# The third batch's layer-0 feed-forward moved into the rotary attention of a four-layer kernel on Trainium2

## The chip, the cores and the metric

The kernel runs on one core of one Trainium2 chip. Five engines work beside each other, each with its own queue of instructions: TensorE (PE), VectorE (DVE), ScalarE (ACT), GpSimd (POOL) and SyncE (SP). The metric is device microseconds for one launch. A profiled execution gives a trace, and the page and the answers made from it; all times of single instructions below come from such a trace.

## What is computed

Four batches of 1024 tokens with 128 channels go through four layers. Every layer has the same frame: half a feed-forward, an attention, half a feed-forward, each added to the residual X. Cut to what matters here:

```python
# layer 0: MoE with 8 experts, two of them for a token (gelu), and a small attention over the heads of one token
# layer 1: dense feed-forward and softmax attention with rotary positions, 16 heads of 8 channels
def _L1_ffn_ref(x, w_gate, w_up, w_down):      # HIDDEN = 384
    h = silu(x @ wg.T) * (x @ wu.T)
    return h @ wd.T
def _L1_attn_ref(x, w_qkv, w_out, b_out):
    q, k = q * cos + rotate_half(q) * sin, k * cos + rotate_half(k) * sin
    attn = softmax(q @ k.T * scale)            # over all 1024 tokens of the batch
    return (attn @ v) @ w_out + b_out
# layer 2: MoE and a linear attention; layer 3: RWKV
```

Each part is applied to the normalized X (mean removed, divided by the standard deviation over the 128 channels). The dense feed-forward (half of it, a factor 0.5) ends the kernel's layer-0 stage: it is the first feed-forward of layer 1, and the program issues it batch by batch as soon as a batch's second MoE is combined. In the program it is called `last`.

## The kernel before

**Data.** X[b] is a tile of 128 channels by 1024 tokens in SBUF for each batch b = 0 to 3. "The third batch" is b = 2; b = 3 is the last. A half is 512 tokens.

**Layer 0 and its planner.** Layers 0, 2 and 3 are written as generators of tasks in lanes (`lanes`). In layer 0 the tasks are `route` (which tokens go to which expert), `experts` (blocks of 128 slots; each loads its expert's weights on SP (L834), gathers tokens on POOL, runs two groups of matmuls and scatters the result on POOL (L878)), `combine` (adds the two experts' results to X), the attention, `last(b)`, and `prepare` (the rotary attention's queries, keys and values of batch 0). The second MoE has a group for each batch. The operations are noted down, not issued: `Score.order` then schedules all of them with a table of estimated costs for each engine, and `play` issues them in this order. All of these have the line L296 in the profile, except where a helper issues by itself (L834 and L878). The order of all five engines in the layer is therefore one plan, and any task that is taken out makes it a different one.

**`last(b)`**, which is `l1_ffn` (L1023), does two halves of: a center matmul (X minus its mean), Square and copy, variance matmuls, square root and reciprocal, four transposes that spread the scale over the tokens (`spread`), the product xn, then for three chunks of 128 hidden channels a gate matmul, `AF.Silu`, an up matmul and a product on DVE, and at the end three down matmuls that accumulate and an addition to X. Each matmul of 512 float32 columns shows as two passes.

**The last batch is treated differently.** `macaron` keeps batch 3's second `combine` out of layer 0 (`self.late`, L1767), and `last` is made for the batches 0 to 2 only. Both run later, inside the rotary attention.

**The rotary attention, `l1_attn`** (L1142). Ahead of its loop, POOL fills the rings of padded queries and keys (`l1_rings`, L1076 and L1080) and the value tiles (L1334), and SP loads the first queries and keys from DRAM (`l1_spread`, L1138). The loop at k runs over 256 steps and 11 more:
- `greatest`, steps 0 to 255: for two pairs of heads each, two score matmuls into a `two` tile (64 rows of contraction, two PSUM buffers) and one maximum on DVE (L1181). A step has two such reduces.
- `shifted` after each eighth step: the maxima are turned by four transposes and written beside the queries.
- `scores`, from step 11 on: the score matmuls again, with the maximum subtracted, into an `s` tile (three PSUM buffers), and the exponential on ACT (L1209).
- `values`, one step later: products with the values; `normalized` at the end of each 8 steps.
- at the end of each step, every generator in `running` is advanced by one piece. `coming` prepares batches 1 to 3 (`l1_prepare`, from step 64b - 61), a piece in every third step; `late` runs, from step 10 on and again a piece in every third step, batch 3's `combine` and its feed-forward `feed`. These, too, take their PSUM from the three `s` buffers.

PE is in program order here; the other engines' instructions are ordered by the framework.

**`feed(b, hf)`** is `last` for half a batch, as ten pieces: the center matmul, Square (L1287) and copy; four variance matmuls with root and reciprocal; the spread and xn; for three chunks a gate piece (matmul, Tanh, and (tanh + 1) times gate in one DVE operation, L1307) and an up piece (matmul and product, L1312); the three down matmuls with the addition to X (L1317). The silu is made of tanh: g (tanh(g/2) + 1) is twice silu(g), and the factor at the end is 0.25, not 0.5. Tanh and the exponential need no change of ACT's function table between them in the trace; Sqrt does.

Of the kernel before, what the change touches and what calls it, by code (L numbers as in the profile page):

```python
# [20 lines left out]
B, S, D = 4, 1024, 128  # L21
# [536 lines left out]
class Macaron:  # L558
# [583 lines left out]
    def l1_attn(self, m, c1, f):  # L1142
# [6 lines left out]
        with ExitStack() as ctx:  # L1149
# [16 lines left out]
            def values_of(n):  # L1166
                b, g4 = n // 4, n % 4
                nc.gpsimd.tensor_copy(
                    va[n % RING][:, :, :, 1 : 1 + HD],
                    self.ring["vd"][b % 2][:, :, 32 * g4 : 32 * g4 + 32].rearrange("p t (h d) -> p t h d", d=HD),  # L1170
                )

            def greatest(unit, pair, nm):
                n, (c, it, h) = unit // 16, (unit // 8, unit % 8 // 2, unit % 2)
                at = (c % 2 * 4 + it) * P
                s = two((P, 2, HALF))
                for j in (1, 0):
                    g = 2 * pair + j
                    self.mm(s[:, j, :], of(qz, n, g)[:, at : at + P], of(kz, n, g)[:, h * HALF : (h + 1) * HALF])
                    yield  # L1180
                v.tensor_reduce(nm[:, it, h, 2 * pair : 2 * pair + 2], s, AX.X, ALU.max, negate=True)  # L1181

            def shifted(chunk, nm):
                top, n = tops[chunk % 2], chunk // 2
                least = self.t(wp, [P, 4, 4], "least")
                v.tensor_tensor(least, nm[:, :, 0, :], nm[:, :, 1, :], ALU.min)
                v.tensor_copy(top[:, :, :, 0].bitcast(F32R), least)
                v.tensor_tensor(top[:, :, :, 1], least, top[:, :, :, 0], ALU.subtract)
                yield
                tp = two((P, HALF))  # L1190
                for i in range(4):
                    nc.tensor.transpose(
                        tp[:, i * P : (i + 1) * P], top[:, i].rearrange("p g r -> p (g r)"), self.c0["ident"]
                    )
                sh = self.t(wp, [P, HALF], "sh", F32R)
                nc.scalar.copy(sh, tp)
                for g in range(4):
                    z = of(qz, n, g)[32:34, chunk % 2 * HALF : (chunk % 2 + 1) * HALF]
                    nc.sync.dma_start(out=z.bitcast(F32), in_=sh[32 * g : 32 * g + 2, :].bitcast(F32))
                yield  # L1200

            def scores(unit, pair, es):
                n, jt, at = unit // 16, unit % 8, unit // 8 % 2 * HALF
                for j in range(2):
                    g = 2 * pair + j
                    o = self.t(p2, [P, HALF], "s")
                    self.mm(o, of(kz, n, g)[:, jt * P : (jt + 1) * P], of(qz, n, g)[:, at : at + HALF])
                    e = es[g] = self.t(wp, [P, HALF], "e", bufs=10)
                    nc.scalar.activation(e, o, AF.Exp, scale=scale)  # L1209
                    yield  # L1210

            def values(unit, o, es, half):
                n, jt = unit // 16, unit % 8
                c = slice(half * HALF // 2, (half + 1) * HALF // 2)
                for g in range(4):
                    self.mm(
                        o[32 * g : 32 * g + 32, c], va[n % RING][:, jt, g, :], es[g][:, c],
                        start=jt == 0 and half == 0, stop=jt == NT - 1 and half == 1,
                    )
# [101 lines left out]
            def chain(*parts):  # L1321
                for first, part in parts:
                    while at < first:
                        yield
                    for _ in part:
                        yield
                        yield
                        yield

            at = -1  # L1330
            late = [(10, part(b, hf)) for part in (combine, feed) for b in self.late for hf in range(2)]
            coming = [(64 * b - 61, self.l1_prepare(p2, "s", prep, m, c1, b)) for b in range(1, B)]
# [6 lines left out]
            running, nms, pending, o = [chain(*coming)], {}, None, None  # L1339
            for k in range(units + LEAD + 1):  # L1340
                at = k
                first = k if k < units else None
                second = k - LEAD if 0 <= k - LEAD < units else None
                if k % 16 == 2 and RING <= k // 16 + 1 < 4 * B:
                    self.l1_spread(k // 16 + 1)
                    values_of(k // 16 + 1)
                if k == 1:
                    running.append(chain(*late))
                if first is not None and first % 8 == 0:
                    nms[first // 8] = self.t(wp, [P, 4, 2, 4], "nm", bufs=3)  # L1350
                es = {}
                for pair in range(2):
                    top = greatest(first, pair, nms[first // 8]) if first is not None else iter(())
                    part = scores(second, 1 - pair, es) if second is not None else iter(())
                    for one in (part, top, top, part, top):
                        next(one, None)
                    if pending:
                        unit, then = pending
                        if unit % 8 == 0 and pair == 0:
                            o = self.t(pa, [P, HALF], "o")  # L1360
                        values(unit, o, then, pair)
                if pending and unit % 8 == 7:
                    running.append(normalized(unit // 8, o))
                pending = (second, es) if second is not None else None
                if first is not None and first % 8 == 7:
                    running.append(shifted(first // 8, nms[first // 8]))
                running = [r for r in running if next(r, self) is not self]
            while running:
                running = [r for r in running if next(r, self) is not self]
# [408 lines left out]
    def layer0(self, moe, m, right, enter, ffn, l1a, c1):  # L1778
        m["wqkvc"] = self.centered(m["wqkv"], 3 * D)
        spare = enter(self.rings, "l1vd", 1)  # L1780
        self.ring["vd"] = [self.t(spare, [P, NT, D], f"vd{i}") for i in range(2)]
        pa, pf = enter(right, "l0a"), enter(right, "l1f0", side="left")
        side = self.side

        def more(route):
            attn = lambda b, *after: (f"middle{b}", after, lambda: self.l0_attn(side, pa, m, b))
            last = lambda b: (f"last{b}", (f"combine1{b}",), ffn(pf, side, b))
            prepare = ("prepare", ("last0",), lambda: self.l1_prepare(side, "bank", pf, l1a, c1, 0))
            return (
                [*[route(0, g) for g in groups[0]], *[attn(b, f"combine0{b}") for b in range(B)]],  # L1790
                [route(1, g, *(f"middle{b}" for b in g)) for g in groups[1]],
                [last(0), prepare, *[last(b) for b in range(1, B - 1)]],
            )

        groups = [(0,), (1,), (2, 3)], [(b,) for b in range(B)]
        marks = {(n, g): f"_{n}{g[0]}" for n in range(2) for g in groups[n]}
        aside = [(0, (1,)), (0, (2, 3)), (1, (0,)), (1, (1,)), (1, (2,))]
        self.macaron("l0", moe, AF.Gelu, groups, marks, more, [(1, B - 1)], aside)
# [112 lines left out]
```

## Time and profile before

| | |
|---|---|
| time, median of 8 runs (range) | 2475.01 us (2468.7 to 2481.79) |
| profiled execution: time | 2474.69 us |
| profiled execution: span, first to last instruction | 2472.9 us |
| mean granted TensorE clock | 0.953 |
| busy: PE, DVE, ACT, POOL | 2193.0, 1766.5, 1546.9, 1093.2 us |
| layer 0 | from 0 to 702.5 us |
| rotary attention, first and last reduce | 703.05 and 1485.7 us |
| layers 2 and 3 | the rest |

The span is what lies between the first and the last instruction; the time of the execution is 1.8 us longer. Busy time is an average over stages in which different engines are full, so the sum says little about one of them: for that, the profile cuts the span into 40 equal slices of 61.8 us (a digit is the busy share in tenths), and windows of any length can be asked for. An idle time in brackets behind an instruction, with an arrow, is how long its engine was idle ahead of it, and what ended that. `out<-in` are the program's names of the tiles.

### The profile page before, as it was taken

The numbers are of one execution on the slowest core, as the hardware profiler recorded it, in microseconds if no ns is written. First come the engines' busy times: TensorE is split into PE (matmuls) and PEld (weight loads), VectorE is DVE, ScalarE is ACT, GpSimd is POOL, SyncE is SP. The second block draws the span as 40 slices with busy tenths as digits, with TensorE's granted clock in tenths as the row PEclk, the third lists the DMA queues.
The fourth block names the chain that finished last, engine by engine and source line by source line (L and its number), as shares of the span: only waits on it lengthen the run. The fifth ranks groups of instructions, "written<-read, shape, count | busy, mean of one in ns | idle before, by whom it ended". The sixth has DMA issues, their size and how long they took to land. (4 is left out here: it accounts for less than half of the span.)

```text
span 2472.9 us, 44544 instructions
## 1 busy us (share of the span) xinstructions
PE 2193.0 (89%) x15631; PEld 1396.8 (56%) x15631; DVE 1766.5 (71%) x2891; ACT 1546.9 (63%) x3903; POOL 1093.2 (44%) x1140
## 2 busy tenths in 40 slices
PE   5879787988979999999999999988998978689986
PEld 4878776776744334334333334578887968433332
DVE  4488979886458887998988992542656542398995
ACT  5567675855537776787788886654554554456643
POOL 2778876578622201210320000077454567255553
PEclk8989998999969999999999999998998989899998
DMA  6977766567731101110220000278666689200000
GB/s 200 294 225 243 227 205 193 161 194 235 229 84 57 53 19 36 55 51 19 69 69 19 25 3 11 74 249 267 217 195 198 207 268 284 81 0 5 5 9 17
DMA packets 135694, 312.40 MB, mean 126 GB/s; under 512 B 20752, under 2 KB 70032, under 8 KB 135344
## 3 DMA queue, kind: packets, MB, share of 16 engines
q1 hardware_dynamic: 110320, 253.28, 31.9%
q0 software_dynamic: 25152, 56.28, 8.2%
q8 instruction: 125, 2.05, 0.3%
q14 instruction: 97, 0.79, 0.1%
HBM read 259.86 MB, written 49.09 MB: 125 GB/s over the span
## 5 line engine op out<-in xcount | busy, mean ns | idle before, releaser
L1181 DVE TENSOR_REDUCE nm<-two 128x2 f32<-128x1024 f32 x512 | 622.9, 1223 | 70.6 <-PE s L601 42.8
L1209 ACT ACTIVATE e<-s 128x512 f32<-128x512 f32 x1024 | 558.2, 598 | 132.9 <-PE s L601 119.3
L296 POOL DMA_INDIRECT e_xg<-rows,g_source x333 | 379.7, 1140 | 437.4 <-DVE g_target L296 221.9
L296 ACT ACTIVATE e_h<-bank,e_w 128x128 f32<-128x128 f32 x1332 | 383.6, 377 | 266.7 <-PE bank L296 113.4
L878 POOL DMA_INDIRECT res<-e_y,g_target x333 | 370.6, 1113 | 184.7 <-issue 45.8
L296 PE MATMUL bank<-e_x,e_w 128*128 128x128 f32 x2664 | 387.3, 286 | 38.5 <-DMA e_w<-in_l0m_dram 22.1
L296 PE MATMUL bank<-e_w,e_h 128*128 128x128 f32 x2664 | 390.5, 283 | 8.9 <-ACT e_h L296 8.9
L601 PE MATMUL s<-qz,kz 64*128 64x512 f32 x1024 | 383.0, 449 | 2.9 <-ACT e L1209 2.9
L296 PEld LDWEIGHTS bank<-e_x,e_w 128*128 128x128 f32 x2664 | 349.0, 200 | 60.0 <-issue 31.9
L601 PE MATMUL two<-kz,qz 64*128 64x512 f32 x1024 | 360.2, 460 | 6.8 <-DVE nm L1181 6.7
L296 PEld LDWEIGHTS bank<-e_w,e_h 128*128 128x128 f32 x2664 | 352.9, 198 | 20.5 <-ACT e_h L296 12.7
L601 PE MATMUL o<-e,va 128*32 128x256 f32 x4096 | 328.7, 392 | 7.6 <-ACT os L1226 7.5
L601 PEld LDWEIGHTS s<-qz,kz 64*128 64x128 f32 x1024 | 157.6, 186 | 205.0 <-issue 98.0
L601 PEld LDWEIGHTS o<-e,va 128*32 128x32 f32 x4096 | 81.6, 108 | 191.9 <-issue 173.6
L1140 POOL MEMSET qz<- 2x1024 f32 x52 | 49.1, 945 | 309.0 <-PE s L601 306.8
L296 ACT ACT_TABLE_LOAD x124 | 159.1, 1283 | 12.8 <-PE bank L296 9.8
L296 PE MATMUL bank<-c,e_xg 128*128 128x128 f32 x333 | 93.6, 292 | 78.8 <-DMA e_xg<-rows,g_source 69.6
L296 DVE TENSOR_TENSOR e_y<-bank,e_w 128x128 f32<-128x128 f32 x202 | 57.5, 286 | 142.5 <-PE bank L296 131.9
L601 PEld LDWEIGHTS two<-kz,qz 64*128 64x128 f32 x1024 | 143.2, 189 | 25.3 <-DVE nm L1181 21.9
L296 DVE COPY e_x<-bank 128x128 f32<-128x128 f32 x162 | 45.8, 286 | 135.6 <-PE bank L296 134.1
L1119 POOL TENSOR_TENSOR h<-h 128x512 f32<-128x512 f32 x12 | 15.4, 1283 | 226.8 <-DVE h L1115 172.5
L296 PEld LDWEIGHTS bank<-c,e_xg 128*128 128x128 f32 x333 | 48.5, 147 | 97.2 <-issue 41.1
(316 smaller groups left out, 3454.3 us busy)
## 6 DMA issues: line engine op xcount, KB each, us to landing
e_w<-in_l0m_dram SPq DMA_DIRECT2D x177, 578.0 KB
e_w<-in_l2m_dram SPq DMA_DIRECT2D x156, 578.0 KB
c_y<-res SPq DMA_DIRECT2D x30, 512.0 KB
stack<-s POOLq DMA_DIRECT2D x48, 256.0 KB
rows<-g_xt SPq DMA_DIRECT2D x16, 512.0 KB
qz<-stack SPq DMA_DIRECT2D x64, 128.0 KB
kz<-stack SPq DMA_DIRECT2D x64, 128.0 KB
e_xg<-rows,g_source POOLq DMA_INDIRECT x333
```

Of the source, the lines that this page charges most:

```text
L296: return call(*a, **k)
L601: self.nc.tensor.matmul(out, lhsT, rhs, start=start, stop=stop)
L878: ins = real.gpsimd.indirect_dma_start(out=res[:, :], out_offset=at(target[:, k : k + 1]), in_=y, in_offset=None)
L1119: nc.gpsimd.tensor_tensor(whole, turned[:, 0, :], turned[:, 1, :], ALU.add)
L1140: self.nc.gpsimd.memset(z[at + 32 : at + 34, :].bitcast(F32), 0.0)
L1181: v.tensor_reduce(nm[:, it, h, 2 * pair : 2 * pair + 2], s, AX.X, ALU.max, negate=True)
L1209: nc.scalar.activation(e, o, AF.Exp, scale=scale)
```

## The change

`last` is made for the batches 0 and 1 only, and a generator `first_feeds` runs `feed` for batch 2, both halves: 20 pieces. It is put into `running` at k = 0 without `chain`, so it is advanced in every step, from step 0 to step 19. The operations are those of `feed` above, so the silu of batch 2 is made of tanh. Batch 3's `late` work keeps its place, and so does the preparation of the batches 1 to 3; batch 2's begins at step 67, which is behind the pieces.

```diff
@@ in l1_attn
+            def first_feeds():
+                for hf in range(2):
+                    yield from feed(B - 2, hf)
+
             at = -1
             late = [(10, part(b, hf)) for part in (combine, feed) for b in self.late for hf in range(2)]
...
                 if k == 1:
                     running.append(chain(*late))
+                if k == 0:
+                    running.append(first_feeds())
@@ in layer0
-                [last(0), prepare, *[last(b) for b in range(1, B - 1)]],
+                [last(0), prepare, *[last(b) for b in range(1, B - 2)]],
```

## The prediction

> **What bounds the kernel now.** I read four views, in this order. First the busy tenths in 40 slices, 61.8 us each, to find which engine is full in which stage.
>
> ```profile
> PE   5879787988979999999999999988998978689986
> DVE  4488979886458887998988992542656542398995
> POOL 2778876578622201210320000077454567255553
> PEclk8989998999969999999999999998998989899998
> L1181 DVE TENSOR_REDUCE nm<-two 128x2 f32<-128x1024 f32 x512 | 622.9, 1223 | 70.6 <-PE s L601 42.8
> ```
>
> Counted from 0, slice 11 (680 to 742 us) is the border of layer 0 and the rotary attention: POOL falls from 6 to 2, and the granted clock is at 6 tenths there and nowhere else. In the rotary attention behind it (slices 12 to 23) PE is at 9 throughout and DVE at 7 to 9. A step of it needs two reduces of L1181 (512 of 1223 ns), and neighbouring reduces start 1.23 us apart when nothing else is there: a bare step is 2.46 us.
>
> Second, the windows around the border: from the end of batch 3's attention of layer 0 (602 us) to rotary step 26, and a late stretch. Columns: stretch, its length, then busy us (instructions) of PE, PEld, DVE, ACT, POOL, the granted clock, the DMA share, GB/s.
>
> ```profile
> 602.00:628.00 26.00, 23.34 (x96) 13.15 (x95) 18.34 (x62) 20.42 (x54) 24.53 (x27) 1.00 0.47 127
> 655.00:687.00 32.00, 25.62 (x211) 23.92 (x210) 5.88 (x23) 15.07 (x55) 23.83 (x29) 0.97 0.92 282
> 687.00:705.00 18.00, 15.72 (x115) 13.49 (x113) 5.56 (x13) 6.75 (x24) 7.84 (x16) 0.95 0.54 151
> 705.00:736.00 31.00, 23.21 (x67) 11.16 (x67) 24.34 (x29) 8.00 (x16) 3.91 (x9) 0.51 0.10 28
> 1100.00:1300.00 200.00, 197.19 (x1726) 79.91 (x1724) 176.08 (x188) 157.81 (x293) 37.77 (x49) 1.00 0.17 51
> ```
>
> From 655 to 687 the transfers are at 0.92: batch 3's expert weights come at the speed of the DMA engines, and PE is idle for 6.4 of 32 us. From 705 to 736 nothing is full, at half the clock: there is room in the first rotary steps, and a clock that makes PE's work cost double. Third, POOL and PE at the end of layer 0:
>
> ```profile
> 632.56 0.99 POOL L296 DMA_INDIRECT e_xg<-rows,g_source  x1 [4.40 <-DVE g_far L296]
> 690.88 0.97 POOL L878 DMA_INDIRECT res<-e_y,g_target  x1 [3.59 <-DVE e_y L296]
> 701.40 0.97 POOL L878 DMA_INDIRECT res<-e_y,g_target  x1 [3.97 <-DVE e_y L296]
> ...
> 685.96 0.45 PE L296 MATMUL bank<-c,e_xg 128*128 128x128 f32 x1 [3.44 <-DMA e_xg<-rows,g_source]
> 699.44 1.13 PE L296 MATMUL bank<-e_x,e_w 128*128 128x128 f32 x8 [1.28 <-DMA e_w<-in_l0m_dram]
> 702.51 1.04 PE L601 MATMUL two<-kz,qz 64*128 64x512 f32 x4
> ```
>
> Each line ends with the idle time before it and what ended it. The rotary attention begins (702.51) right behind the last expert matmul, and what PE waits for on the way there is a gather, then a weight; no wait is on the feed-forward that moves. Last, DVE in the first rotary steps:
>
> ```profile
> 703.05 9.14 DVE L1181 TENSOR_REDUCE nm<-two 128x2 f32<-128x1024 f32 x8
> 713.55 6.88 DVE L1181 TENSOR_REDUCE nm<-two 128x2 f32<-128x1024 f32 x6 [1.36 <-PE two L601]
> 721.79 3.48 DVE L1181 TENSOR_REDUCE nm<-two 128x2 f32<-128x1024 f32 x3 [1.36 <-PE two L601]
> ...
> 728.93 2.35 DVE L1181 TENSOR_REDUCE nm<-two 128x2 f32<-128x1024 f32 x2 [1.22 <-PE two L601]
> 734.00 1.23 DVE L1181 TENSOR_REDUCE nm<-two 128x2 f32<-128x1024 f32 x1 [2.72 <-PE two L601]
> ```
>
> Eight reduces follow each other without a gap: even here, where neither exp nor values run, the reduces set the pace (2.26 us a step). Each idle time of DVE stands where a background piece of batch 1's preparation held up PE (a center matmul 1.36 each, the transposes 1.22, the sixteen variance passes 2.72).
>
> **What the change removes in layer 0.** The feed-forward of batch 2 is 18 matmuls (592 ns at the median, two passes each, 0.86 us from start to start: 15.5 us), two center matmuls (1.7), the variance passes (2.0) and the spreads (1.7): about 21 us of PE, with ten DVE operations of 0.69 us and ten ACT operations of about 0.6. Its PE work lies at 619 to 656, its late down matmuls at 654.5, 686.2 and 695.6. The Silu table loads (1283 ns each) go too; they lie on ACT beside waits.
>
> How much earlier the last expert matmul comes depends on what else is late. The whole of layer 0 is ordered anew by its planner. Comparing the two orders of instructions: in the changed kernel DVE has 498.4 us of work ahead of the last attention's addition to X (493.0 before), and 16.9 us from there to the last routing's g_source (25.5 before), so the routing is ready sooner. But POOL has 10 scatters and a gather of batch 2 left at that point, where before it had 2 scatters: 9 more operations at 1.27 us (0.97 and a 0.30 us issue gap), 11.4 us. The 24 ring fills of POOL (0.95 us each) stand there as before: all ahead of batch 3's first gather, 19 of them in the changed order. So:
> - If POOL's queue decides: between 602 and 704.9 it has 20.0 us of idle gaps longer than 0.6 us. All of them filled, with 11.4 us of work added, it ends 8.6 us sooner. If the gaps stay as they are, less the 11.4 us that fill them, it ends when it ended: 0.
> - If PE's queue decides: 21 us sooner.
> - Transfers are for the first: at 0.92 of the DMA engines, 32 us of this stretch cannot be shortened by taking PE work from it; and 20 of the first 24 loads of qz and kz now stand behind the last weight on SP (6 before), 128 KB each. At 282 GB/s one takes 0.46 us, and the first reduce needs four, so up to 2 us, which I leave in the bounds.
> I take **-7 us** for layer 0, next to the POOL bound; bounds 0 and -21.
>
> **What it adds in the rotary attention.** Twenty pieces, one a step, at steps 0 to 19. A step's length is the distance between the first reduces of neighbouring steps. The trace has the same function for batch 3, later, at full clock; steps with one of its pieces and nothing else, less the bare 2.46: center 3.52 (+1.06), variance 3.77 (+1.31), the step after it with the table back 3.90 (+1.44), spread 3.03 (+0.57), gate 4.32 and then 2.27 (+1.67), up 3.52 (+1.06), the three downs 5.24 (+2.78). One half of the batch: 1.06 + 1.31 + 1.44 + 0.57 + 3 x 1.67 + 3 x 1.06 + 2.78 = 15.35 us.
>
> Second half of the batch, steps 10 to 19. Scores begin at step 11, so that row applies: +15.35. Step 12 is 5.32 us now, because the four spreads of batch 1's preparation run at half clock; step 30 has the same spreads at full clock in 3.05. With 128-row matmuls in steps 3 to 10 the clock may be back by then: -2.3. If center and variance at steps 10 and 11, ahead of the scores, find room as in the first half, another 2.4 goes. I take **+13** (10.7 to 15.4).
>
> First half, steps 0 to 9, which take 31.0 us now (703.0 to 734.0). No row shows these pieces here, so two bounds. If the clock stays full, PE has the room: two reduces take 2.26 us and the four passes of a step about half of it. What counts is DVE: eight operations of 0.69 and a reciprocal of 0.19 are 5.7 us, and the DVE idle times shown above, 1.36 + 1.36 + 1.22 + 2.72 = 6.7 us, would go, since they come from PE at half clock: about 0. If the clock is half throughout, each of the ten big matmuls costs what the center matmul costs at step 3 (3.70 - 2.27 = 1.43), 14.3, and the variance and spread pieces about 2.4: +17. What does the clock do? The window 702.4 to 705.8 has PE busy for 1.94 of 3.40 us, and from 705.8 the clock is 0.50; a window with 1.99 of 3.40 inside layer 0 (589.8 to 593.2), filled by full-height matmuls, keeps 1.00. So the 64-row matmuls of the reduces seem to count for less, and the added 128-row pieces could hold the clock part of the time. I take the middle, **+8**.
>
> A rule of the Trainium skill stands against the row here. Its page "TensorE: Matmul & The Clock Gate", section "HAM oscillation — how this bites in real kernels", lets the clock fall only after PE has been idle for over some 3.4 us; in the trace the longest idle time of PE ahead of the fall is 0.78 us, and it falls. By the rule the clock would stay full, the first half would cost nothing, and the sum would be +6 instead of +14; the measurement decides.
>
> **Sum.** -7 + 8 + 13 = +14 us. The profiled run took 2474.69 us (span 2472.9), the median of the eight runs is 2475.01: the same within 0.4 us. Forecast 2489 us. After step 20 the order of instructions is unchanged, and so is what follows; nothing there gives the time back, because from there on PE is busy for 197 of 200 us.
>
> **Rivals.**
> 1. *Faster.* Layer 0's end is bound by PE's queue and the routing ahead of it, not by POOL. For: the routing's g_source has 8.6 us less DVE work ahead of it, and the first gather (632.56) waited 4.40 us for that chain; DVE is idle from 590.7 to 601.3 ahead of the last addition. Against: the DMA share of 0.92 and the 11.4 us on POOL. Price: the 21 us of PE work and those 4 to 8.6 us, 25 to 30 off layer 0, and +21 in the rotary attention: 2475 - 6 = 2469. It decides from the point where the first rotary matmul starts before 702.5 - 21 = 681.5 us.
> 2. *The clock holds.* The added matmuls keep the clock up from step 0: the first half costs nothing, the second its low end. -7 + 0 + 11 = +4: 2479. For: the full-height window above. Against: of the pieces of steps 0 to 2, where the clock falls, only the center matmul is big.
> 3. *Half clock and no gain.* POOL's added work eats all of layer 0's gain, and the clock stays low to step 12: 0 + 17 + 13 = +30: 2505. For: the slice with clock 6, and 19 x 0.95 + 11.4 = 29.5 us of POOL work ahead of batch 3's gathers. Against: 20 us of POOL's idle time.
> That the pieces don't run where they are put can be excluded: the order on PE, which is manual here, has them at steps 0 to 19.
>
> **Chances.** Forecast (+8 to +22) 0.50; faster 0.22; the clock holds 0.16; half clock and no gain 0.12. This kernel's measurement tells about 0.2% (5 us) from no change. Of the faster case 0.04 lies within that, of the clock case 0.11, the rest of it above: faster 0.18, same 0.15, slower 0.67. The range: the bounds of the sum are -21 + 0 + 11 = -10 (2465) and 0 + 17 + 15 = +32 (2507). I let it reach from 2465 to 2503; left out are the rest of rival 1 (0.08) and the upper part of rival 3 (0.07). The forecast's own range is 2483 to 2497.
>
> **What would show it.** Right: the first rotary matmul at 693 to 699 us; the first reduce of step 20 some 83 us behind the first rotary matmul (62.5 now); gaps of POOL ahead of the scatters smaller than now. Wrong: the first rotary matmul before 681 (rival 1); a granted clock over 0.9 from the start to step 10 (rival 2); the start at 702 or later with the clock at 0.5 past step 12 (rival 3). Also wrong would be a difference in the profile behind step 25, where I cost nothing.

## The result and the profile after

The changed kernel takes **2491.07 us** at the median of 15 runs (2485.35 to 2497.25); the kernel before takes 2474.98 us beside it (43 runs). The ratio is 1.0066, with a 95% interval of 1.0055 to 1.0076: 16 us slower. The forecast was 2489 us. The sum came out within 2 us; its term for layer 0 did not, as the trace shows.

The profiled execution took 2494.53 us (span 2492.7), 3.5 us over its median, where that of the kernel before lay on its median. So of the 19.8 us between the two spans some 3.5 are chance. First the slices of the page:

```profile
PE   5888887978789999999999999997997978689986
DVE  4487899795268887888998992552656652398995
POOL 2778776566822201220220000067554567255553
PEclk7999988989889999999999999999998989899998
L1181 DVE TENSOR_REDUCE nm<-two 128x2 f32<-128x1024 f32 x512 | 623.2, 1222 | 67.6 <-PE s L601 45.7
```

Slice 11 (now 686 to 748 us) no longer stands out: the granted clock is at 8 tenths there, not 6. The reduces cost what they cost. Slice 10 of POOL is at 8 (it was 6): its queue is full ahead of the border. Then the windows. The columns are stretch, length, busy us (instructions) of PE, PEld, DVE, ACT and POOL, clock, DMA share, GB/s:

```profile
602.00:628.00 26.00, 24.08 (x204) 21.97 (x203) 14.97 (x61) 17.71 (x68) 23.47 (x31) 1.00 0.85 259
628.00:633.00 5.00, 0.00 (x0) 0.00 (x0) 0.00 (x0) 0.00 (x0) 4.66 (x6) 0.71 0.76 268
633.00:655.00 22.00, 15.28 (x101) 14.34 (x102) 2.34 (x9) 7.84 (x29) 17.80 (x21) 0.73 0.53 147
655.00:687.00 32.00, 25.51 (x186) 24.09 (x186) 9.09 (x30) 13.84 (x48) 25.24 (x30) 0.87 0.90 285
```

The second line carries the reading of layer 0: for 5 us PE, DVE and ACT do nothing at all, and POOL alone works. What it works on, and who waits for it, the timelines of DVE, POOL and PE show:

```profile
625.54 0.23 DVE L296 SCALAR_TENSOR_TENSOR g_source<-g_w,g_far 128x23 uint32<-128x23 f32 x1
...
626.72 0.95 POOL L1080 MEMSET kz<- 32x1024 f32 x1
627.83 0.96 POOL L878 DMA_INDIRECT res<-e_y,g_target  x1 [0.16 <-issue]
629.00 2.90 POOL L1080 MEMSET kz<- 32x1024 f32 x3
632.07 0.96 POOL L878 DMA_INDIRECT res<-e_y,g_target  x1 [0.17 <-issue]
633.07 0.95 POOL L1080 MEMSET kz<- 32x1024 f32 x1
634.17 0.98 POOL L296 DMA_INDIRECT e_xg<-rows,g_source  x1 [0.16 <-issue]
...
636.71 0.48 PE L296 MATMUL bank<-c,e_xg 128*128 128x128 f32 x1 [9.09 <-DMA e_xg<-rows,g_source]
...
702.89 0.73 PE L601 MATMUL two<-kz,qz 64*128 64x512 f32 x4
```

The last routing is ready at 625.5 us, 6.6 us sooner than before (632.1). But its first gather is issued at 634.17, behind ring fills and batch 2's last scatters in POOL's queue; before, it came at 632.56. PE waits 9.09 us for it, and the first rotary matmul comes at 702.89 us, where it was 702.51. **Layer 0 has gained nothing.**

In the rotary attention (steps counted from the first reduce; 703.43 us now) the steps 0 to 9 take 34.8 us, where they took 31.0, and the steps 10 to 19 take 42.0, again for 31.0. Together +14.8. From step 20 to the last reduce it is 721.9 for 720.7. The DVE timeline of the first steps:

```profile
703.43 5.75 DVE L1181 TENSOR_REDUCE nm<-two 128x2 f32<-128x1024 f32 x5
709.09 0.17 DVE L1296 RECIPROCAL frstd<-fstd 128x4 f32<-128x4 f32 x1
...
710.29 0.67 DVE L1301 TENSOR_TENSOR f_xn<-f_xc,s 128x512 f32<-128x512 f32 x1
710.88 4.78 DVE L1181 TENSOR_REDUCE nm<-two 128x2 f32<-128x1024 f32 x4
715.58 0.68 DVE L1307 SCALAR_TENSOR_TENSOR f_s<-f_t,s 128x512 f32<-128x512 f32 x1
...
729.20 2.36 DVE L1181 TENSOR_REDUCE nm<-two 128x2 f32<-128x1024 f32 x2 [0.65 <-PE two L601]
...
734.14 0.20 DVE L1101 RECIPROCAL p_r<-p_std 128x8 f32<-128x8 f32 x1 [1.53 <-ACT p_std L1100]
737.60 0.69 DVE L1317 SCALAR_TENSOR_TENSOR x<-s,x 128x512 f32<-128x512 f32 x1 [3.26 <-PE s L601]
```

To 729 us DVE stands without a gap, between reduces and the pieces' own operations: the center matmuls at steps 3 and 6, each of which stopped it for 1.36 us before, stop it no more, since the clock is at 1.0. (In a second profile of the same kernel the clock was at 0.5 in just these two steps, and they took 4.1 and 4.2 us, not 2.4 and 2.9.) Only at step 9, where the clock has fallen to 0.5, PE holds it up again: sixteen variance passes of batch 1's preparation and the six passes of the first three down matmuls stand one behind the other.

### The profile page after: what moved, and what is told of

Read it like the earlier page. It is cut to its first block, busy times and chain, and to the rows that moved or that the text cites. A ratio compares the mean times of both kernels' runs of the same rounds, so it can differ in the third digit from the quotient of the medians.

```text
span 2492.7 us, 44539 instructions
## 1 busy us (share of the span) xinstructions
PE 2205.1 (88%) x15631; PEld 1409.3 (57%) x15631; DVE 1769.7 (71%) x2905; ACT 1549.7 (62%) x3900; POOL 1090.8 (44%) x1126
## 5 line engine op out<-in xcount | busy, mean ns | idle before, releaser
L296 POOL DMA_INDIRECT e_xg<-rows,g_source x333 | 370.7, 1113 | 443.5 <-DVE g_target L296 226.9
L296 PE MATMUL bank<-e_x,e_w 128*128 128x128 f32 x2664 | 395.1, 289 | 19.3 <-DMA e_w<-in_l0m_dram 5.7
L296 PE MATMUL bank<-e_w,e_h 128*128 128x128 f32 x2664 | 395.6, 285 | 9.4 <-ACT e_h L296 9.1
L296 PEld LDWEIGHTS bank<-e_x,e_w 128*128 128x128 f32 x2664 | 357.1, 204 | 38.0 <-issue 10.8
```

The lines of the kernel that those rows point to most:

```text
L296: return call(*a, **k)
```

## The experiments

The theory after the result (A): what the pieces cost in the rotary attention is the whole loss, since layer 0 can't end sooner while POOL's queue holds batch 3's gathers back; and the pieces were cheap in steps 0 to 9 because they keep the clock up. The rivals were that layer 0 had become faster and something else ate it (B); that the expert weights and not POOL bound its end (C); that POOL's queue bound it in the kernel before as well (D); and that the clock has another cause (E). The first four kernels ran on a chip on which the kernel before takes 2594.14 us; on the others it takes 2473.5 to 2476.2. On the first chip the kernel before itself was not profiled. In the four profiles from there the first rotary matmul comes at 739.6 to 749.1 us and not at 688 to 703, while the steps 0 to 19 of a rotary attention without the pieces take the same time (61.5 us with the layer 0 of before): what is slower there is outside the rotary attention.

**Layer 0 alone.** Batch 2's feed-forward is left out of layer 0 and not put anywhere.

```diff
-                if k == 0:
-                    running.append(first_feeds())
```

> The changed layer 0 with nothing added to the rotary attention: batch 2's feed-forward at the end of layer 0 is left out of the computation altogether. Theory A (layer 0 gained nothing, because POOL's queue holds batch 3's gathers back; the whole loss is in the rotary attention): the first rotary matmul again near 703 us, steps 0 to 19 as in the kernel before, 62 us, so 2475 us, within 4 us. Rival B (taking 21 us of PE work out does shorten layer 0, and the changed kernel's profiled run only did not show it, or the added pieces themselves delay the border): 2462 to 2470 us.

Measured: 2597.71 us, ratio 1.0015 (1.0000 to 1.0030): no gain, though a loss of up to 8 us isn't excluded. Once more on a chip of 2473.5 us:

> Once more the changed layer 0 with nothing added to the rotary attention; batch 2's feed-forward at the end of layer 0 is left out of the computation. On a chip on which the kernel before takes some 2475 us, Theory A (the narrow ring fills on POOL hold batch 3's gathers back): batch 3's first gather again 8 to 9 us behind its g_source, the first rotary matmul at 699 to 704 us, 2472 to 2478 us. Rival B (without the pieces layer 0 ends sooner): 2468 us or less.

Measured: 2475.68 us, ratio 1.0009 (0.9998 to 1.0021). First gather 8.6 us behind g_source (621.95 and 630.59), first rotary matmul at 701.25 us, steps 0 to 19 in 62.6 us. With a whole feed-forward taken out of the program the time stays what it was. B falls: there is no gain that something ate.

**The pieces alone.** Layer 0 keeps batch 2's feed-forward, and the pieces run as well, so batch 2 gets it twice.

```diff
-                [last(0), prepare, *[last(b) for b in range(1, B - 2)]],
+                [last(0), prepare, *[last(b) for b in range(1, B - 1)]],
```

> The layer 0 of before, with batch 2's feed-forward in it, and the twenty pieces in the rotary attention as well, so that batch 2 gets this feed-forward twice. Theory A: the loss is the pieces': steps 0 to 19 take 77 us, not 62, and the time is 2475 + 15 = 2490 us, within 3 of the changed kernel. Rival B (part of the loss comes from the re-ordered layer 0 and from the later loads of queries and keys): 2480 to 2486 us.

Measured: 2608.65 us, ratio 1.0053 (1.0036 to 1.0070), 14.5 us over the kernel before on the slower chip. In the trace the steps 0 to 9 take 36.5 us and the steps 10 to 19 take 42.0, 17.1 more than the 61.5 us of the kernel with the wide fills below, which ran beside it with the rotary steps of before. The steps are A's; the time alone leaves room for B, since the interval of the ratio is 9 to 18 us there, and B's upper end was 11. The two halves of the change add up within their intervals: 0.0009 to 0.0015 for the one, 0.0053 for the other, 0.0066 for both.

**Wide fills.** Each ring tile is filled in one memset of all 128 rows; the loads write their rows over it.

```diff
-                for j in range(2):
-                    fill.memset(z[64 * j + 32 : 64 * j + 64, :].bitcast(F32), value)
+                fill.memset(z[:, :].bitcast(F32), value)
```

A memset of 128 rows takes 0.96 us, as one of 32 rows does, so POOL has 12 fills less. In the changed kernel, on the slower chip:

> The changed kernel, with each ring tile of queries and keys filled by one memset of all 128 rows, not by two of 32 rows: 12 fills of about 0.98 us (the row of the value tiles' fill) and not 24 of 0.95, so 11 us less on POOL ahead of batch 3's gathers. Theory A (POOL's queue bounds the end of layer 0): the first gather of batch 3 comes at 627 to 630 us and not 634, the first rotary matmul 4 to 9 us sooner, 2482 to 2487 us. Rival C (the expert weights bound it, DMA share 0.90 from 655 to 687 us): no change, 2491 us.

Measured: 2614.81 us, ratio 1.0067 (1.0041 to 1.0093). The changed kernel itself was not run on that chip, but nothing there speaks for a gain: the ratios of its two halves, 1.0015 and 1.0053, add up to the same, and the first rotary matmul comes at 749.1 us, where it came at 739.6 with the same layer 0 and narrow fills. On a faster chip, with the changed kernel beside it:

> The changed kernel itself, as a control on the chip of this call, since the last call's chip takes 2594 us for the kernel before and not 2475. Both theories: 14 to 18 us over the kernel before of this call; steps 0 to 19 take 76 to 79 us.

> The changed kernel with 12 wide ring fills for 24 narrow ones, once more beside the changed kernel. Theory A (POOL's queue bounds the changed layer 0 where weights come fast): if the kernel before takes some 2475 us on this chip, 4 to 9 us under the changed kernel, with batch 3's first gather at 627 to 630 us. Rival C (the weights bound it): the same as the changed kernel within 3 us; on a chip on which the kernel before takes some 2594 us both expect this.

Measured: 2491.45 us for the changed kernel, ratio 1.0054 (1.0036 to 1.0072), and 2480.98 us with wide fills, 1.0021 (1.0007 to 1.0034): **10.5 us less** by the medians, 8 by the ratios. Its POOL timeline, where g_source was ready at 622.75:

```profile
617.95 0.97 POOL L878 DMA_INDIRECT res<-e_y,g_target  x1 [0.19 <-issue]
618.91 0.12 POOL L552 MEMSET idle<- 128x1 f32 x1
621.78 0.95 POOL L878 DMA_INDIRECT res<-e_y,g_target  x1 [2.75 <-DVE g_lanes L296]
623.70 0.98 POOL L296 DMA_INDIRECT e_xg<-rows,g_source  x1 [0.96 <-PE bank L296]
```

The fills are gone from this stretch, POOL has idle time again, and the gather follows the routing within 1 us. It comes 7.0 us sooner than in the changed kernel beside it, and the first rotary matmul 9.9 us sooner (689.9 for 699.8 us). Over all profiles on the faster chips: with the changed layer 0 and narrow fills it came at 696.2 to 702.9 us (five profiles, mean 700.0), with wide fills at 688.2 to 689.9 (three profiles), with the layer 0 of before at 702.5 and 697.2. So the feed-forward's place in layer 0 is worth some 11 us, and POOL's queue had hidden all of it. C falls for these chips (on the first chip nothing speaks against it): that the transfers, at a DMA share of 0.90, hold this end where it is, as the prediction argued too, is refuted. They may still set how long the stretch behind the first gather takes (64 to 71 us to the first rotary matmul in these ten profiles), but the stretch begins with that gather. What sets its length was not tested.

In the kernel before, on the first chip:

> The same wide fills in the kernel before. Theory A: POOL had been idle 4.4 us ahead of batch 3's first gather there, which waits for the routing (g_far), and so less POOL work changes nothing: 2475 us within 3. Rival D (POOL's queue bounds the end of layer 0 in both kernels, so the change isn't what made it the bound): 4 to 9 us less, 2466 to 2471 us.

Measured: 2595.25 us, ratio 1.0001 (0.9982 to 1.0019). The gap of POOL ahead of the first gather is 4.40 us in the kernel before, on a faster chip. On this chip, with the layer 0 of before and narrow fills (the kernel of the pieces alone), and then with wide fills:

```profile
652.65 11.80 POOL L1080 MEMSET kz<- 32x1024 f32 x12
669.20 0.99 POOL L296 DMA_INDIRECT e_xg<-rows,g_source  x1 [4.74 <-DVE g_far L296]
```

```profile
645.14 5.43 POOL L1079 MEMSET kz<- 128x1024 f32 x6
666.22 0.99 POOL L296 DMA_INDIRECT e_xg<-rows,g_source  x1 [15.66 <-DVE g_far L296]
```

The time taken from POOL becomes idle time (10.9 us more of it), because there the routing is late, not the queue. D falls on this chip, where wide fills gained nothing in the changed kernel either. On the faster chips, where the same 11 us of POOL work are worth 8 to 10.5 us in the changed kernel, the kernel before was not run with wide fills. That they would be worth nothing there is argued from POOL's idle time ahead of the first gather: 4.40 us in the kernel before, and 4.75 in the same layer 0 on that chip (in the kernel of the next experiment).

**Holding the clock.** The kernel before, with a matmul a step that nobody reads:

```diff
+                if k < 13:
+                    self.mm(self.t(p2, [P, HALF], "s"), self.c0["center"], self.X[0][:, 0:HALF])
                 running = [r for r in running if next(r, self) is not self]
```

> The kernel before with one more 128-row matmul at the end of each of the steps 0 to 12, whose result nobody reads. Theory A (the added pieces hold the granted clock up, because full-height matmuls count for it; the 64-row ones of the reduces don't suffice): the clock stays at 1.0 from 705 us on, the idle times of DVE in steps 3 to 12 mostly go, these steps take 6 to 9 us less, and the kernel is 4 to 9 us faster than the kernel before. Rival E (the clock of the changed kernel's first steps has another cause, such as what layer 0 does just before): the clock falls to 0.5 as before, each added matmul costs up to 1.43 us, and the kernel is 5 to 18 us slower.

Measured: 2471.91 us, ratio 0.9983 (0.9966 to 1.0000): 4.3 us faster, at the edge of what can be told. Steps 0 to 9 and 10 to 19 of the kernel before, and then of this one (the clock is the third number from the end):

```profile
703.05:734.00 30.95, 22.68 (x66) 10.94 (x67) 24.29 (x27) 6.02 (x13) 5.67 (x12) 0.54 0.11 32
734.00:765.00 31.00, 30.37 (x226) 12.12 (x228) 27.63 (x33) 22.81 (x43) 1.90 (x3) 0.85 0.04 10
```

```profile
697.80:725.40 27.60, 23.59 (x86) 9.74 (x86) 24.39 (x28) 7.01 (x16) 5.64 (x12) 1.00 0.12 35
725.40:756.70 31.30, 29.51 (x232) 11.54 (x234) 27.66 (x32) 21.84 (x40) 1.89 (x2) 1.00 0.04 10
```

More matmuls (86 passes for 66), the clock at 1.00 throughout, and the first ten steps are 3.4 us shorter, with the same DVE work: E falls. Whether the height of the added matmuls does it, or only that PE has more to do, this run can't tell. Steps 10 to 19 gain nothing (31.3 for 31.0), although step 12 went from 5.3 to 4.0; step 17 took that back (4.6 us for 3.2), for a cause that was not followed up. Against A's 6 to 9 us, the steps 0 to 19 are 3.0 us shorter, and the rotary attention as a whole 1.4 us (781.2 for 782.6). What is left of the 4.3 us the rotary attention doesn't explain.

**Two pieces a step**, so that all are done ahead of the scores:

```diff
-                    running.append(first_feeds())
+                    running.extend([first_feeds()] * 2)
```

> The changed kernel with two pieces a step, so that all twenty are done by step 9, ahead of the first scores of step 11. Theory A (a piece costs little ahead of the scores and its full price beside them): steps 10 to 19 take 31 to 33 us as in the kernel before, steps 0 to 9 some 39 to 43; 3 to 8 us faster than the changed kernel, 8 to 12 over the kernel before. Rival F (PE, with 1.0 us for the four passes of a step and 1.7 for two pieces, over the 2.26 us of two reduces, becomes the bound, and the pieces wait for each other): steps 0 to 9 take 48 us or more, no better than the changed kernel.

Measured: 2485.60 us, ratio 1.0045 (1.0029 to 1.0060). That is 5.9 us under the changed kernel beside it by the medians, but only 2 by the ratios (1.0045 and 1.0054), whose intervals overlap: that it is faster as a whole isn't shown. The steps are clearer:

```profile
696.70:740.37 43.67, 35.46 (x131) 15.55 (x129) 34.75 (x47) 19.29 (x32) 4.95 (x10) 1.00 0.19 54
740.37:768.85 28.48, 26.55 (x226) 10.56 (x227) 27.24 (x33) 20.90 (x39) 1.94 (x3) 1.00 0.04 11
```

At full clock throughout, the first ten steps carry the whole feed-forward in 43.7 us, and the second ten take 28.5. That is 10.2 us over the kernel before for all twenty pieces (72.1 for 62.0), where the changed kernel paid 14.8 and, in its second profile, 22.1. F's 48 us were not reached, and PE is busy for 35.5 and DVE for 34.8 of the 43.7 us, so neither sum binds; A's own numbers (39 to 43 and 31 to 33) were missed on both sides, and PE stands idle for 8 us.

**Pieces beside the scores**, from step 20 on, with batch 3's late work begun at step 40:

```diff
-            late = [(10, part(b, hf)) for part in (combine, feed) ...
+            late = [(40, part(b, hf)) for part in (combine, feed) ...
-                if k == 0:
+                if k == 20:
                     running.append(first_feeds())
```

> The changed kernel with the twenty pieces at steps 20 to 39, where scores, exponentials and values run, and batch 3's late work begun at step 40, not 10, so that the two don't meet. Theory A (beside the scores each piece costs what batch 3's pieces cost, 15.35 us a half): steps 0 to 19 as in the kernel before, 62 us; steps 20 to 39 some 28 to 31 us more than in it less what batch 3's work there cost (some 13 us, which comes later in its place); 2475 + 31 = 2506 us, about 14 us over the changed kernel. Rival G (the pieces cost the same everywhere, since DVE's and PE's work is the same): 2491 us, as the changed kernel.

Measured: 2497.96 us, ratio 1.0095 (1.0082 to 1.0108): 24.5 us over the kernel before and some 8 over the changed one. G falls, but A was too high: from the first reduce to the last this rotary attention takes 808.1 us, 25.4 more than that of the kernel before (782.6), where 31 were expected. So a piece beside the scores costs less in a row of pieces than a lone one of batch 3's did: an up piece behind a gate piece makes a step of 2.96 us where no other background piece runs (steps 26, 34 and 38), not 3.52.

**Halves side by side.** Wide fills, and both halves as generators of their own, in steps 0 to 9; the second half's tiles are the buffers of the exponentials, which stand idle until step 11:

```diff
-            def feed(b, hf):
+            def feed(b, hf, own=""):
...
-                one = lambda tag, bufs=1: self.t(wp, [P, HALF], tag, bufs=bufs)
+                one = lambda tag, bufs=1: self.t(wp, [P, HALF], "e" if own else tag, bufs=10 if own else bufs)
...
-                    running.append(first_feeds())
+                    running.extend([feed(B - 2, 0), feed(B - 2, 1, "b")])
```

> The changed kernel with the wide ring fills, and with the two halves of batch 2 as two generators, each advanced once a step: both run in steps 0 to 9, ahead of the first scores, and each piece has a whole step until the next one of its half. The second half's tiles are of the exponentials' buffers, which are idle until step 11. Theory A (ahead of the scores PE has the room; what a piece costs there is the wait of PE's queue for the result of the piece before): steps 0 to 9 take 33 to 38 us (43.7 with two dependent pieces a step), steps 10 to 19 some 29 to 31, layer 0 ends 10 us sooner than in the changed kernel: 2464 to 2472 us, under the kernel before, if the kernel before takes some 2475 us on this chip; on a chip with slow weights 0 to +6 us against it. Rival F (PE's and DVE's sums bound these steps): steps 0 to 9 take 43 us or more, 2476 us or more.

Measured: 2472.72 us, ratio 0.9995 (0.9984 to 1.0007): the same as the kernel before. Layer 0 ends at 688.2 us, as expected; but the steps 0 to 9 take 42.4 us, not 33 to 38, and F's 43 are all but reached. Steps 0 to 8 take 30.6 of these, 2.6 to 4.7 each, and step 9 takes 11.8: sixteen variance passes and twelve passes of down matmuls stand in a row, most of them at half clock, since PE was busy for only 0.52 of the 3.4 us from 716.5 on, and the clock fell behind them, at 719.9. The last kernel adds matmuls that nobody reads at the steps where the clock fell:

```diff
+                if k in (7, 8, 10, 11, 12):
+                    self.mm(self.t(p2, [P, HALF], "s"), self.c0["center"], self.X[0][:, 0:HALF])
```

> The kernel of wide fills and halves side by side, with one more 128-row matmul, whose result nobody reads, at the end of the steps 7, 8, 10, 11 and 12, where its trace shows the granted clock falling to 0.5 (from 719.9 and from 733.6 us). Theory A (what is left of the pieces' price is the clock: step 9 with six down matmuls and sixteen variance passes takes 11.8 us at half clock, step 12 takes 5.3): the clock stays at 1.0, step 9 takes some 7 to 9 us and step 12 some 4, 4 to 6 us less than without; 0.9970 to 0.9985 of the kernel before, faster than both kernels. Rival H (the steps 9 and 12 are bound by their chains of ACT and DVE, not by the clock): no gain, or up to 4 us slower by the added matmuls.

Measured: 2470.98 us, ratio 0.9991 (0.9978 to 1.0004). The PE timeline of step 9 without them, and with them:

```profile
720.03 3.67 PE L601 MATMUL s<-c,sq 128*128 128x64 f32 x16
723.49 4.42 PE L601 MATMUL s<-f_h,l1f_wd 128*128 128x512 f32 x6
727.75 2.74 PE L601 MATMUL s<-e,l1f_wd 128*128 128x512 f32 x6
```

```profile
720.95 2.00 PE L601 MATMUL s<-c,sq 128*128 128x64 f32 x16
722.78 2.79 PE L601 MATMUL s<-f_h,l1f_wd 128*128 128x512 f32 x6
725.41 2.74 PE L601 MATMUL s<-e,l1f_wd 128*128 128x512 f32 x6
```

The variance passes go from 3.67 to 2.00 us and the first downs from 4.42 to 2.79; step 9 takes 8.5 us, step 12 takes 4.0 (5.3), and the steps 0 to 19 are 4.2 us shorter (69.1 for 73.3). So that step was bound by the clock, as A had it, and H falls. The first ten steps still take 39.1 us at full clock, more than the 33 to 38 that were expected of halves side by side; what holds them there stays open. The two kernels ran on different chips; by their ratios to the kernel before (0.9995 and 0.9991) the 4.2 us can't be seen in the whole time. By the ratios to the kernel before (0.9991 and 1.0066) this version is some 19 us faster than the changed kernel; that it beats the kernel before is not shown, as its interval reaches over 1.

## Why the prediction was right, and where it was not

- **Layer 0: -7 us forecast, 0 measured.** This term failed, at the step "All of them filled, with 11.4 us of work added, it ends 8.6 us sooner". Most of the gaps were filled (20.0 us of them became 7.4), but that is a sum over the whole stretch, and what counts is where the queue stands when the routing is ready. The prediction had the numbers for it and used them only in its third rival: 19 fills and nine operations, 29.5 us, and the two scatters that had been there, 2.5, put behind 602 us give 634.0. The first gather came at 634.17. (To 0.2 us this is partly luck: the trace has 20 fills, not 19, and nine gathers and scatters there.) Since it came at 632.56 before, nothing was left to gain. That layer 0 can end sooner, by some 11 of the 21 us of the other bound, shows once POOL's queue is shortened.
- **First half: +8 forecast, +3.8 in the profiled run, +8.3 in the second profile of the same kernel** (39.3 for the 31.0 of before), +2.1 to +5.6 in three other kernels with the same steps; the mean of the five is +5.1, so the middle between the two clock cases was some 3 us too high. The reason was right: the clock was held part of the time, and the price goes with it. The five profiles give +2.1 us at a mean clock of 0.95 over these steps, +3.8 at 0.90, +5.6 at 0.86 (twice) and +8.3 at 0.78.
- **Second half: +13 forecast, +11.0 measured** (+13.8 in the second profile). Step 12 came to 4.4 us with two pieces in it (7.8 in the second profile, at half clock). Against the same steps of the kernel before, the gate pieces of steps 13, 15 and 17 added 1.7, 1.4 and 1.5 us in the first profile, for the 1.67 of the row, and the three downs 3.0 for 2.78. The up pieces of steps 14, 16 and 18 added 0.5, 0.5 and 0.2, where the row of a lone piece said 1.06 each: this term was 2 us too high, which is what the half was off by.
- **The sum: +14 forecast, +16.1 measured.** The layer's term was 7 us too hopeful and the rotary terms together 6 us too high by the first profile (+14.8 for +21). Two errors stood against each other, so that the sum came so close is luck. By the second profile (+22.1 for the pieces, with layer 0 ending 2.8 us sooner than in the one profile of before) the pieces' sum was nearly exact; over the five profiles with these steps it is +14.6 to +22.1, with a mean of 16.9.
- **The signs.** The first rotary matmul was to come at 693 to 699 us if the steps were right; it came at 702.9 and 699.7. The first reduce of step 20 was to follow it by some 83 us; it did by 77.3 and 84.6. Of rival 3 the first half happened (POOL's work eats the gain) and of rival 2 nearly the second (the clock mostly holds). The break-even point of rival 1, a rotary start ahead of 681.5 us, was not reached even with wide fills (688.2).
- **Behind step 25 nothing was costed.** The two profiles differ by 1.2 us from step 20 to the last reduce, and by 3.4 us behind it. The order is the same, and the eight other profiles on faster chips give 987.5 to 997.2 us for that last stretch (987.2 and 990.7 in these two; 990.5 with the layer 0 of before, in the kernel that holds the clock). So the difference lies within what other executions show, and it needs no cause in the change.
- **The rule on the clock.** The prediction set the row (the clock falls after PE was idle for 0.78 us at most) over the rule of the Trainium skill ("TensorE: Matmul & The Clock Gate", section "HAM oscillation — how this bites in real kernels"), which is to have no idle gaps of PE over some 3.4 us. That the clock stays full without such gaps was the prediction's reading of it. The runs side with the row: in fifteen falls of the clock in the first 75 us of the rotary attention, over ten profiles, PE's longest idle time in the window of 3.4 us ahead of the fall was 0.63 to 1.66 us.

## What to carry to other kernels

An engine's queue in order is read at the moment that matters: add up what stands in it behind a known point until the instruction that others wait for, and compare that with when its data are ready; its total of idle time doesn't tell this. Work taken off an engine that is waited for can come to nothing because another queue moves up to the same time, and small work that fills a queue with nobody waiting (here two memsets for one) is free until the day a change makes it late. Background work was cheap ahead of the busy stage and dear in it (the twenty pieces cost 10.2 us there at full clock, and 25.4 beside the scores), and matmuls that nobody needs can shorten steps in which the clock would otherwise fall (here by 3 to 4 us over twenty steps; that the whole kernel gains by it isn't shown).

## What the runs showed of the hardware that was not expected

- **The clock went with how much 128-row work PE had, not with long idle times.** Every stretch of one granted clock in the traces lasts a whole multiple of 3.41 us. In such windows at full clock, in the first 75 us of the rotary attention, with PE busy for less than 0.85 (ten profiles), the clock fell after those 15 in which matmuls of 128 rows, transposes left out, filled 0 to 0.33 (median 0.06), whatever the 64-row ones added (up to 0.58). It stayed after those 37 in which they filled 0.19 to 0.82 (median 0.42). With the transposes counted, the falls reach to 0.40 (median 0.19). A window with 0.71 busy, 0.53 of it at 64 rows, lost the clock; one with 0.54 busy, 0.34 of it at 128 rows, kept it. The ranges overlap, so this is no exact bound, and the share that PE is busy with anything sorts the windows nearly as well: a cut at 0.59 has 5 of the 52 on the wrong side, a cut at 0.22 of the 128-row share 3. The kernels that held the clock added work and height at once. That the height decides is likely, not shown.
- **The same program met this differently in two executions**: the two profiles of the changed kernel have a clock of 0.90 and 0.78 in steps 0 to 9 and take 34.8 and 39.3 us for them.
- **A POOL memset of 32 rows took as long as one of 128**: 0.95 and 0.96 us for 1024 float32 a row.
- **Chips differed outside the rotary attention**: with the layer 0 of before the first rotary matmul came at 739.9 and 748.9 us on one chip and at 702.5 and 697.2 on faster ones, and the rotary steps 0 to 19 without the pieces took 61.5 us there and 62.0 in the kernel before.
